# Double batches of leftover matmuls, and a beginning with whole loads on one queue

## The chip, the cores and the metric

The kernel runs on one core of a Trainium2 chip. The metric is device time in microseconds (us) of one execution; six executions of the kernel before took 2045.05 to 2046.72 us, with a median of 2046.22. The core has five engines with a queue each that run side by side: PE (TensorE, matmuls and weight loads), DVE (VectorE), ACT (ScalarE), POOL (GpSimd) and SP (SyncE, which here only issues DMAs; ACT issues some too).

## The reference

The input x has 4096 rows, 32 fields and 16 numbers per field. Two layers follow each other. Each forms all products of two fields, mixes them with a weight matrix, adds a bias, and normalizes each output channel over rows and numbers:

```python
def _cin_layer(out, x, W, b, gamma, beta):
    r, _, e = x.shape
    h = jnp.einsum('rne,rfe->rnfe', out, x).reshape(r, -1, e)
    h = jnp.einsum('rce,oc->roe', h, W) + b[None, :, None]
    return _batchnorm(h, gamma, beta)
h1 = _cin_layer(x, x, W1, b1, g1, beta1)
out, direct1 = (h1[:, :64], h1[:, 64:])
direct2 = _cin_layer(out, x, W2, b2, g2, beta2)
agg = jnp.concatenate([direct1, direct2], axis=1)
return agg.sum(axis=-1)
```

W1 is 128 x 1024 (32 x 32 field pairs), W2 is 128 x 2048. The mean and the variance of layer one are needed before layer two can multiply, so the two layers are two stages of the kernel.

## The kernel before

The change lies in stage one alone, which is layer one; it fills the first 490 of the 2043 us. The 65,536 columns (rows times numbers) are cut into 128 tiles of 512 columns; `t` counts them, and `s = t % GROUP` is the place in a group of eight.

Because both operands of a pair are x, the pairs (i, j) and (j, i) share one product, and their weights are added once at the start: `w1_sb = w1_sb + w1m_sb` on POOL (L312), in pieces of one, one, two and two of six chunks. A tile needs four products of 128 partitions by 512 columns (the main part, `z`, chunks m = 0 to 3) and 16 products of fields that lie 16 apart (the leftovers). The leftovers fill only 32 partitions for a tile, so those of four tiles are packed into one 128-partition array: one load `r` per group holds the leftovers of all eight tiles of the group (32 partitions hold two tiles, and the weight chunks 4 and 5 have zeros for the other one), and DVE multiplies it once to `zr` (L373, `leftovers`).

For each tile the work goes like this:
- SP issues the loads of `a` and `b` (512 KB each, L294 in `load_main`), one tile ahead in the text; four buffers of each mean that the loads of tile t wait until DVE has used tile t - 4. The first tile's loads are in halves. The weights `w1` and `w1m` are loaded on ACT's queue (L308, L309).
- DVE multiplies `z = a * b` (L387 `multiply_main`; the first two tiles by chunks, L396 `multiply_chunk`). There are four buffers of `z`.
- PE runs four matmuls on `z` with `w1_sb` into one PSUM bank (L428), 128 rows and 128 columns of weights each.
- At tiles with s = 0 and s = 4 PE first runs `add_leftovers` (L380): four matmuls of 32 rows each, in four different row groups, one for each of the next four tiles. They start the accumulation in these four banks. The first two tiles are the exception: they get theirs at the end (`begun`).
- `finish(t - 1)`, in the text right behind tile t's matmuls, evicts the bank of the tile before: ACT writes `e` with the bias (L352), DVE takes its statistics (L115), ACT writes the half that layer two needs (`kept`, L355, stored to DRAM by a DMA on ACT's queue) and the half that is only summed (`ed`, L358); every second tile DVE sums `ed` (L364 `sum_direct`).

PSUM has eight banks. Stage one takes six for the tiles (`psum`, bufs=6); the other two (`factors`) hold the warm-up and are used in stage two. Buffers of one: `r` and `zr`. Buffers of two: `e` and `ed`.

The order on each engine's queue is drawn up by the framework from the dependences and from the order in which the text emits the instructions: of those that it reckons ready, the one emitted first goes first. So a product can stand ahead of statistics that are emitted earlier but ready later (in the trace the product of tile 40 stands ahead of the statistics of tile 36). Where the text has `issue_after(x)`, the instruction comes behind x on its engine. Once drawn up, each queue runs strictly in order.

Some work for stage two is mixed in by tile number: the weights of layer two (load at t = 6, combined by DVE at t = 20), differences of fields (`EARLY`: loads at 14 + 24g, negated and summed on ACT and DVE behind it, stored at 37 + 24g), and the first loads of stage two (t = 75, 83, 91, 99, 107, 115).

The last four tiles (`ENDING`) are done by halves of the output channels, the half that layer two needs first, so that its statistics can be finished (L505 to L519 on DVE and ACT), while PE does the other half (L461). `add_leftovers_halves` adds their leftovers from the group's `zr` with chunk 5. A small matmul `keep_ps` spreads the scale and shift over partitions (its operand is `blocks`, L519), and stage two begins (L698).

Before all this PE runs `BEGIN` = 3 matmuls on ones (L239), whose result nobody reads, while the first loads are on their way.

## Time and profile before

| what | value |
|---|---|
| median of six executions | 2046.22 us |
| the profiled execution | 2045.05 us |
| its span, first to last instruction | 2043.3 us |
| mean granted clock of PE | 0.998 of full |
| PE busy | 2027.5 us |
| DVE busy | 1959.0 us |
| POOL busy, nearly all in stage two | 1486.4 us |
| first matmul on a tile | 8.22 us |
| end of main matmuls of tile 123 | 474.1 us |
| begin of stage two on PE | 490.48 us |

The page lists the busy time of each engine, then the chain that ended last: from the last instruction back to what released it, again and again, so that the shares show which engine set the end. Below it stand groups of instructions by line with their count, busy time, mean ns of one, and how long the engine was idle before them and who ended that. PE is the matmuls, PEld the weight loads that run beside them. In the records, a matmul of f32 shows as two, because it goes over the array in two passes, and the name `w_sb` stands for `w1_sb` in stage one. "xN" is a count of records. A DMA's time to landing includes its wait in the queue.

### The profile page before, as it was taken

The page shows a single profiled execution, that of the slowest core. Times are in us where ns is not written, and L with a number is a line of the kernel's source. Part 1 is how long each engine was busy: PE and PEld are TensorE (multiplying, and loading weights), DVE is VectorE, ACT ScalarE, POOL GpSimd, SP SyncE. Part 2 cuts the span into 40 slices and gives each one's busy share as a digit, 9 for nine tenths or more (in the row PEclk, how much of TensorE's full clock was granted, in tenths as well). Part 3 has the DMA queues.
Part 4 walks back from the last instruction along what each step waited for, and adds up shares of the span by engine and source line. Part 5 has one row for each costly group of instructions (what it writes and reads, how often), then busy time and mean ns, then how long its engine had stood idle before and what let it go on. Part 6 is the DMA issues. An engine that isn't in the chain of part 4 may idle for free.

```text
span 2043.3 us, 24467 instructions
## 1 busy us (share of the span) xinstructions
PE 2027.5 (99%) x8500; PEld 885.3 (43%) x8500; DVE 1959.0 (96%) x1521; ACT 1186.1 (58%) x1914; POOL 1486.4 (73%) x525
## 2 busy tenths in 40 slices
PE   9999999999999999999999999999999999999997
PEld 3444444443344444444444444444444444444443
DVE  8998987998999999999999999999999999999997
ACT  4555554554566666655665656556656565566564
POOL 0000000002999999999999999999999999999996
PEclk9999999999999999999999999999999999999999
DMA  9999999996777777777776777777767777777661
GB/s 391 379 346 371 348 359 355 358 390 188 176 176 181 174 175 180 190 174 188 174 177 166 174 173 178 175 183 177 176 167 174 173 173 183 181 177 175 169 162 42
DMA packets 112380, 440.70 MB, mean 216 GB/s; under 512 B 13056, under 2 KB 13056, under 8 KB 103808
## 3 DMA queue, kind: packets, MB, share of 16 engines
q1 hardware_dynamic: 105840, 418.43, 73.6%
q10 hardware_dynamic: 6416, 20.72, 2.7%
q8 instruction: 66, 1.08, 0.2%
q14 instruction: 58, 0.48, 0.1%
HBM read 417.07 MB, written 22.02 MB: 215 GB/s over the span
## 4 chain that ended last, share of the span: by engine, by line
PE 98%; DVE 1%; issue 0%; POOL 0%; DMA 0%; ACT 0%; DVEq 0%; ACTq 0%; POOLq 0%
PE x L698 74%; PE ps L428 21%; PE ps L380 2%; PE ps L461 1%; DMA w1m_sb<-in_w1m 0%; POOL t L714 0%; DVE zz L667 0%; DVE d L934 0%; ACT u L659 0%; DVE both L662 0%; POOL t L703 0%; ACT both L659 0%; DVE d L833 0%; DVE t L662 0%; POOL w_sb L312 0%
## 5 line engine op out<-in xcount | busy, mean ns | idle before, releaser
L714 POOL TENSOR_TENSOR t<-zz,t 128x2048 f32<-128x2048 f32 (+1 forms) x260 | 1163.0, 4474 | 20.6 <-DVE t L662 0.9
L698 PE MATMUL x<-t,s_sb 128*64 128x512 f32 x2040 | 958.3, 592 | 0.4 <-POOL t L714 0.4
L698 PE MATMUL x<-zz,s_sb 128*64 128x512 f32 x2048 | 934.8, 592 | 0.0
L698 PE MATMUL x<-zz,w_sb 128*64 128x512 f32 x2056 | 760.2, 592 | 0.0
L703 POOL TENSOR_TENSOR t<-zz 128x512 f32<-128x512 f32 x255 | 327.1, 1283 | 516.8 <-DVE zz L667 516.3
L667 DVE TENSOR_TENSOR zz<-f,bx 128x2048 f32<-128x2048 f32 x255 | 582.3, 2283 | 19.7 <-ACT f L659 19.7
L659 ACT ACTIVATE f<-a,keep 128x512 f32<-128x512 f32 x512 | 398.2, 778 | 342.6 <-DVE zz L667 294.7
L667 DVE TENSOR_TENSOR zz<-f,b 128x2048 f32<-128x2048 f32 x255 | 582.3, 2284 | 0.1
L698 PEld LDWEIGHTS x<-t,s_sb 128*64 128x64 f32 x2040 | 279.2, 137 | 486.2 <-issue 457.6
L698 PE MATMUL x<-t,w_sb 128*64 128x512 f32 x1020 | 479.3, 592 | 0.0
L428 PE MATMUL ps<-z,w_sb 128*128 128x512 f32 x992 | 434.7, 596 | 1.3 <-POOL w_sb L312 1.2
L698 PEld LDWEIGHTS x<-zz,s_sb 128*64 128x64 f32 x2048 | 279.5, 137 | 247.8 <-issue 240.3
L387 DVE TENSOR_TENSOR z<-a,b 128x2048 f32<-128x2048 f32 (+1 forms) x127 | 288.2, 2270 | 43.0 <-PE ps L428 20.6
L428 PEld LDWEIGHTS ps<-z,w_sb 128*128 128x128 f32 x992 | 185.7, 190 | 248.9 <-issue 228.6
L698 PEld LDWEIGHTS x<-zz,w_sb 128*64 128x64 f32 x2056 | 238.9, 137 | 121.4 <-issue 119.4
L659 ACT ACTIVATE b<-zz 128x512 f32<-128x512 f32 x255 | 152.5, 598 | 187.1 <-DVE zz L667 187.0
L352 ACT ACTIVATE e<-ps,bn_sb 128x512 f32<-128x512 f32 x124 | 85.2, 687 | 214.7 <-PE ps L428 167.5
L662 DVE TENSOR_TENSOR t<-zz,b 128x512 f32<-128x512 f32 x255 | 173.3, 680 | 0.4
L698 PEld LDWEIGHTS x<-t,w_sb 128*64 128x64 f32 x1020 | 139.6, 137 | 0.0
L596 ACT ACTIVATE unread<-e,center 128x512 bf16<-128x512 f32 x122 | 86.3, 707 | 0.0
L358 ACT ACTIVATE ed<-ps,bn_sb 64x512 f32<-64x512 f32 x124 | 84.8, 684 | 2.3
L115 DVE BATCH_NORM_STATS2 stats<-e 128x6 f32<-128x512 f32 x124 | 84.9, 686 | 0.0
(103 smaller groups left out, 867.5 us busy)
## 6 DMA issues: line engine op xcount, KB each, us to landing
a<-h SPq DMA_DIRECT2D x256, 512.0 KB, 4.6
b<-in_xb SPq DMA_DIRECT2D x64, 1024.0 KB, 9.4
a<-in_xa SPq DMA_DIRECT2D x127, 512.0 KB, 7.2
b<-in_xb SPq DMA_DIRECT2D x127, 512.0 KB, 8.2
bx<-in_xb SPq DMA_DIRECT2D x64, 512.0 KB, 9.3
bx<-x SPq DMA_DIRECT2D x64, 512.0 KB, 10.9
h<-kept ACTq DMA_DIRECT2D x64, 256.0 KB, 5.7
r<-in_xr SPq DMA_DIRECT2D x16, 512.0 KB, 8.9
```

The source lines that it names most:

```text
L115: nc.vector.bn_stats(self.stats[:, self.at, :], h)
L352: nc.scalar.activation(e, ps, AF.Identity, bias=b1)
L358: done = nc.scalar.activation(ed[to, :], ps[KEEP:, :], AF.Identity, bias=b1[KEEP:])
L387: return nc.vector.tensor_tensor(z[:, k], a.rearrange("p (a t) -> p a t", a=2)[:, k].unsqueeze(2).to_broadcast([P, n, 2, T]), b.rearrange( ...
L428: nc.tensor.matmul(pss[t], w1_sb[:, m, :], z[:, m // 2, m % 2, :], start=t < FIRST and m == 0, stop=t >= FIRST and m == 3,)
L596: return nc.scalar.activation(unread, e[:, s], AF.Square, bias=center[:, s], accum_out=squares[:, s, c : c + 1])
L659: return queue("act", lambda: nc.scalar.activation(to, source, AF.Identity, **scale_bias))
L662: return dve(lambda: nc.vector.tensor_tensor(to, x, y, ALU.add))
L667: dve(lambda: nc.vector.tensor_tensor(z, a, b.rearrange("p (k q) t -> p k q t", k=2), ALU.mult))
L698: queue("pe", lambda: nc.tensor.matmul(self.of[x], w, b, start=start, stop=stop))
L703: queue("pool", lambda: nc.gpsimd.tensor_tensor(t2[:, 0], z[:, 1, 0], z[:, 0, 0], ALU.add))
L714: queue("pool", lambda: nc.gpsimd.tensor_tensor(t14[:, k, q], z[:, 2 + k.start : 2 + k.stop, q], twice[:, k, q], ALU.subtract))
```

## The change

The leftovers of tiles 8g - 4 to 8g - 1 and of tiles 8g to 8g + 3 are now added in one go, at tile 8g: eight matmuls behind each other. The first four end the accumulation of tiles that have had their main matmuls (`ends_with_leftovers`), the second four start that of tiles that are to come. The packing of `xr` on the host is moved by four tiles to fit, with a 17th group for the last four tiles; their leftovers are multiplied in the ending, and use chunk 4. As tiles now stay open longer, they use all eight banks (`bank`: six of `psum`, and the two of `factors` for the tiles with t % 8 = 6 and 7), and they are evicted four tiles later: `finish(t - 4)` in place of `finish(t - 1)`, with two at tiles 120 and 121 and `finish(t - 2)` at 122 and 123. The load of the next `r` moves from s = 4 to s = 1 (and to t = 3 for the second one).

At the beginning, the first tile's loads are whole like all others. The weights of both orders of a pair come in one array, `w1_both` (four main chunks, 512 KB) and `left_both` (two chunks of leftovers, 256 KB), loaded on SP's queue: a and b of tile 0, main weights, a and b of tile 1, weights of leftovers, then `r`. DVE adds chunk 0 behind its first product; POOL adds chunk 1, then 2 and 3, then the leftovers'. There are four warm-up matmuls in place of three.

```diff
--- before.py
+++ after.py
@@ -60,7 +61,7 @@
 LAST = 4
 STAGES = (3, 0, 1, 2)
 DIFF = 16
-BEGIN = 3
+BEGIN = 4
 
 FIRST = 2
 
@@ -282,34 +283,17 @@
         def load_main(t):
             a = lpool.tile([P, 2 * T], FP, tag="a", name="a")
             b = lpool.tile([P, 2 * T], FP, tag="b", name="b")
-
-            def load(to, part, n):
-                at = part * T
-                if to is a:
-                    at += xa.offset + t * FIELDS * 2 * T
-                    source = bass.AP(xa.tensor, at, [[2 * T, FIELDS], [0, 4], [1, n * T]])
-                else:
-                    at += xb.offset + (t * WRAP + 2) * T
-                    source = bass.AP(xb.tensor, at, [[T, FIELDS], [4 * T, 4], [1, n * T]])
-                return nc.sync.dma_start(to[:, part * T : (part + n) * T], source)
-
-            if t == 0:
-
-                parts = ((a, 0, 1), (b, 0, 1), (b, 1, 1), (a, 1, 1))
-            else:
-                parts = ((a, 0, 2), (b, 0, 2))
-            for part in parts:
-                last = load(*part)
-            loads.append(last)
+            nc.sync.dma_start(
+                a, bass.AP(xa.tensor, xa.offset + t * FIELDS * 2 * T, [[2 * T, FIELDS], [0, 4], [1, 2 * T]])
+            )
+            at_b = bass.AP(xb.tensor, xb.offset + (t * WRAP + 2) * T, [[T, FIELDS], [4 * T, 4], [1, 2 * T]])
+            loads.append(nc.sync.dma_start(b, at_b))
             return a, b
 
         w1_sb = wpool.tile([P, 6, P], FP, tag="w1", name="w1_sb")
-        w1m_sb = zpool.tile([P, 6, P], FP, tag="z", name="w1m_sb")
-        nc.scalar.dma_start(w1_sb, w1)
-        nc.scalar.dma_start(w1m_sb, w1m)
-
-        for k in (slice(0, 1), slice(1, 2), slice(2, 4), slice(4, 6)):
-            nc.gpsimd.tensor_tensor(w1_sb[:, k], w1_sb[:, k], w1m_sb[:, k], ALU.add)
+
+        w1_both = zpool.tile([P, 2, 4, P], FP, tag="z", name="w1_both")
+        left_both = zpool.tile([P, 2, 2, P], FP, tag="z", name="left_both")
         bn_sb = load_bn()
         w2_sb = const.tile([P, 16, P], FP, tag="w2", name="w2_sb")
         s_sb = const.tile([P, 4, 4, 2, KEEP], FP, tag="s", name="s_sb")
@@ -368,18 +352,28 @@
                 ALU.add,
             )
 
+        def multiply_leftovers(zr, r):
+            return nc.vector.tensor_tensor(zr, r[:, :T], r[:, T:], ALU.mult)
+
         def leftovers(r):
             zr = rpool.tile([P, T], FP, tag="zr", name="zr")
-            nc.vector.tensor_tensor(zr, r[:, :T], r[:, T:], ALU.mult)
+            multiply_leftovers(zr, r)
             return zr
 
-        def add_leftovers(t, zr, begun=0):
+        def bank(t):
+            pool, tag = (psum, "ps") if t % GROUP < 6 else (factors, "f")
+            return pool.tile([P, T], FP, tag=tag, name="ps")
+
+        def ends_with_leftovers(t):
+            return t % GROUP >= 4 or t < FIRST
+
+        def add_leftovers(t, zr):
 
             for k in range(4):
                 rows = slice(32 * k, 32 * (k + 1))
-                nc.tensor.matmul(
-                    pss[t + k], w1_sb[rows, 4 + t % GROUP // 4, :], zr[rows, :], start=k >= begun, stop=k < begun
-                )
+                last = ends_with_leftovers(t + k)
+                w = w1_sb[rows, 4 + (t + 4) % GROUP // 4, :]
+                nc.tensor.matmul(pss[t + k], w, zr[rows, :], start=not last, stop=last)
 
         def multiply_main(z, a, b, k):
 
@@ -396,11 +390,19 @@
             return nc.vector.tensor_tensor(z[:, k, j], a[:, to[0]], b[:, to[1]], ALU.mult)
 
         ending = NT - ENDING
-        main = [load_main(t) for t in range(FIRST)]
+
+        main = [load_main(0)]
+        nc.sync.dma_start(w1_both, w1)
+        main += [load_main(t) for t in range(1, FIRST)]
+        nc.sync.dma_start(left_both, w1_left)
+        for k in (slice(1, 2), slice(2, 4)):
+            nc.gpsimd.tensor_tensor(w1_sb[:, k], w1_both[:, 0, k], w1_both[:, 1, k], ALU.add)
+        nc.gpsimd.tensor_tensor(w1_sb[:, 4:], left_both[:, 0], left_both[:, 1], ALU.add)
         r = load_rem(0)
         for t in range(NT - ENDING):
             s = t % GROUP
-            if s == 4 and t + 4 < NT:
+            if s == 1 and t > 1 or t == 3:
+
                 r = load_rem(t // GROUP + 1)
             if FIRST <= t + 1 < NT:
                 main.append(load_main(t + 1))
@@ -411,6 +413,9 @@
                 for k in range(2):
                     for j in range(2):
                         product = multiply_chunk(z, *main[0], k, j)
+                        if t == k == j == 0:
+                            with tc.issue_after(product.ins):
+                                nc.vector.tensor_tensor(w1_sb[:, 0], w1_both[:, 0, 0], w1_both[:, 1, 0], ALU.add)
             else:
 
                 for k in (slice(0, 1), slice(1, 2)) if t == FIRST else (slice(0, 2),):
@@ -421,27 +426,34 @@
                     zr = leftovers(r)
             if s % 4 == 0:
                 for k in range(4):
-                    pss[t + k] = psum.tile([P, T], FP, tag="ps", name="ps")
-            if s % 4 == 0 and t > 0:
+                    pss[t + k] = bank(t + k)
+            if s == 0 and t > 0:
+                add_leftovers(t - 4, zr)
                 add_leftovers(t, zr)
             for m in range(4):
                 nc.tensor.matmul(
                     pss[t],
                     w1_sb[:, m, :],
                     z[:, m // 2, m % 2, :],
-                    start=t < FIRST and m == 0,
-                    stop=t >= FIRST and m == 3,
+                    start=ends_with_leftovers(t) and m == 0,
+                    stop=not ends_with_leftovers(t) and m == 3,
                 )
             if t == FIRST - 1:
-                add_leftovers(0, zr, FIRST)
-            if t > 0 and t < ending - 1:
-                evicted = finish(t - 1)
+                add_leftovers(0, zr)
+
+            if t >= ending - 2:
+                evicted = finish(t - 2)
+            elif t >= ending - 4:
+                for done in range(2 * t - ending, 2 * t - ending + 2):
+                    evicted = finish(done)
+            elif t >= 4:
+                evicted = finish(t - 4)
             if t == 20:
                 combine_weights()
                 b1_swapped = const.tile([P, 1], FP, tag="b1s", name="b1_swapped")
                 for x, y in ((low, high), (high, low)):
                     nc.scalar.activation(b1_swapped[x], b1[y], AF.Identity)
-            if t == 0:
+            if t < 4:
                 continue
             with tc.issue_after(loads[-1].ins), tc.issue_after(product.ins), tc.issue_after(evicted.ins):
                 if t == 12:
@@ -477,7 +489,7 @@
             for k in range(ENDING):
                 rows = slice(32 * k, 32 * (k + 1))
                 to = banks[k][half_of[(k + direct) % 2]]
-                matmul(to, w1_sb[rows, 5, half_of[direct]], zr[rows, :], k not in begun, k in begun)
+                matmul(to, w1_sb[rows, 4, half_of[direct]], zr[rows, :], k not in begun, k in begun)
 
         zs = []
         for k in range(ENDING):
@@ -485,6 +497,9 @@
                 main.append(load_main(ending + k + 1))
             zs.append(zpool.tile([P, 2, 2, T], FP, tag="z", name="z"))
             queue("dve", lambda: multiply_main(zs[k], *main.pop(0), slice(0, 2)))
+            if k == 0:
+                zr = rpool.tile([P, T], FP, tag="zr", name="zr")
+                queue("dve", lambda: multiply_leftovers(zr, r))
 
         with tc.issue_after(lasts["dve"].ins):
             for t in (ending - 2, ending - 1):
@@ -965,8 +980,10 @@
     n = np.arange(FIELDS)
     xa = np.stack([xt, xt[:, (n + 2) % FIELDS]], axis=2)
     xb = xt[:, np.arange(WRAP) % FIELDS]
-    xr = np.stack([xt[:, :16], xt[:, 16:]], axis=2).reshape(NT // GROUP, GROUP // 4, 4, 16, 2, T)
-    xr = xr.transpose(0, 2, 1, 3, 4, 5).reshape(NT // GROUP, P, 2, T)
+
+    xr = np.stack([xt[:, :16], xt[:, 16:]], axis=2)
+    xr = np.concatenate([xr[:4], xr, xr[-4:]]).reshape(NT // GROUP + 1, GROUP // 4, 4, 16, 2, T)
+    xr = xr.transpose(0, 2, 1, 3, 4, 5).reshape(NT // GROUP + 1, P, 2, T)
 
```

## The prediction

> **What bounds the kernel now.** I read the page first, for the engine that carries the span.
>
> ```profile
> span 2043.3 us, 24467 instructions
> PE 2027.5 (99%) x8500; PEld 885.3 (43%) x8500; DVE 1959.0 (96%) x1521; ACT 1186.1 (58%) x1914; POOL 1486.4 (73%) x525
> PE 98%; DVE 1%; issue 0%; POOL 0%; DMA 0%; ACT 0%; DVEq 0%; ACTq 0%; POOLq 0%
> ```
>
> PE is busy 99% and the chain that ended last is 98% PE. So a gain has to be PE time, and a loss has to be a hole in PE. Next I read the chain in order of time over the first 60 us, where all changed lines lie (the same pattern runs to 474 us).
>
> ```profile
> 1.29 5.25 DMA w1m_sb<-in_w1m
> ...
> 8.22 1.10 PE ps L428 x2
> 9.39 1.10 PE ps L428 x2
> 10.53 5.39 PE ps L428 x12
> 15.91 1.07 PE ps L380 x8
> 16.98 7.06 PE ps L428 x16
> ...
> 25.12 13.93 PE ps L428 x32
> 39.05 1.07 PE ps L380 x8
> 40.12 13.93 PE ps L428 x32
> ```
>
> Each f32 matmul gives two records, its two passes. From 10.53 us on PE has no hole: 32 records of main matmuls, then 8 of leftovers, again and again, 15.00 us per four tiles. The main records start 0.429 us apart (median of 924). 32 x 0.429 = 13.73, so a batch of leftovers costs 15.00 - 13.73 = 1.27 us. Its four matmuls sit in four row groups and run side by side, which is two passes, 0.86 us; the other 0.41 us is the price of going from full rows to 32-row groups and back. Then the weight loads of one batch:
>
> ```profile
> 38.98 0.31 PEld L380 LDWEIGHTS ps<-zr,w_sb 32*128 32x128 f32 x8 [0.76 <-issue]
> ```
>
> All eight loads, those of the second pass too, are over 0.31 us after the first started, while the first pass still runs in the same row groups. Last, DVE, which feeds PE (groups of lines by shape, 60 to 474 us; its waits to 520 us; the timelines at 355 us).
>
> ```profile
> L387 DVE TENSOR_TENSOR z<-a,b 128x2048 f32<-128x2048 f32 x112 | 256.2, 2288 | 41.0 <-PE ps L428 19.4 <-DMA b<-in_xb 17.6 <-PE ps L380 3.6
> L115 DVE BATCH_NORM_STATS2 stats<-e 128x6 f32<-128x512 f32 x111 | 76.2, 687 | 0.0
> L364 DVE TENSOR_REDUCE d<-ed 128x32 f32<-128x512 f32 x56 | 37.5, 669 | 0.0
> L373 DVE TENSOR_TENSOR zr<-r 128x512 f32<-128x512 f32 x14 | 9.4, 670 | 0.0
> ```
> ```profile
> 355.08 8.42 PE L428 MATMUL ps<-z,w_sb 128*128 128x512 f32 x19
> ```
> ```profile
> 355.22 2.29 DVE L387 TENSOR_TENSOR z<-a,b 128x2048 f32<-128x2048 f32 x1 [3.55 <-PE ps L380]
> ```
>
> Eight tiles cost DVE 8 x 2.288 + 8 x 0.687 + 4 x 0.669 + 0.670 = 27.2 us of PE's 30.0. Mostly DVE waits for a free z buffer and is 9 us ahead (the product of tile 40 ends at 151.09, PE starts that tile at 160.06). The thin places are the start (tile 8: 38.36 against 40.05) and tile 93: counted off, the product in the last row is tile 93's, it ends at 357.51, and PE starts the tile eight records after 355.08, at 358.62: 1.1 us. Around it the DMA share is 1.00 (330 to 360 us).
>
> **The change, part by part.**
>
> *Double batches.* Before there are 32 batches, each with its two switches; after, one single batch at tile 1, 15 double ones at tiles 8 to 120, and the ending's own: 15 pairs of switches fewer. A double batch is four passes and one pair of switches if its second half follows as the second pass of a batch follows the first: 4 x 0.429 + 0.41 = 2.13 us, against 2 x 1.27 = 2.54. That is 15 x 0.41 = **-6.1 us**. The least gain, if the joint of the halves costs a half switch (0.2 us), is 15 x 0.2 = 3.1 us.
>
> The Trainium skill, "TensorE: Matmul & The Clock Gate", Part 3, speaks against the joint: a weight load overlaps running matmuls only where its row group differs, and the second half's loads go to the row groups in use. "TensorEngine Tiling (Array Packing)", Key Properties, has only a change of tiling mode drain the array, which speaks for it. By the first I would estimate the smaller gain. The row above shows loads into groups in use, so I take the larger.
>
> *Evictions four tiles late.* Tiles whose number modulo 8 is 4 to 7 are complete only at the next double batch. Then ACT has four of them at once: 4 x 2.04 us (0.687 + 0.670 + 0.684) = 8.2 us, and DVE gets 4 x 0.687 + 2 x 0.669 = 4.1 us of their statistics and sums, ahead of the next product in its queue if they stand in the order of emission. From the batch to the end of the fourth tile behind it PE takes about 15 us; in that time DVE has four products (9.2), eight statistics and four sums (8.2), some 17 us. So in this half DVE falls back from 9 us of lead to, worked out with ACT's pace, about 3.5 us, and in the other half, which has almost only products (four in 14 us), it comes back. In the steady state this is hidden by the lead. Where the lead is gone already it is not: from tile 80 to 93 PE now saves 3 x 1.27 - 2.13 = 1.7 us against a lead of 1.1, a hole of 0.6. At the start tile 4 comes 1.27 us earlier for want of its batch, against leads of 1.7 to 2.5 up to tile 11; no hole by these numbers. For the burst of statistics meeting a late load I add 0.9. **+1.5 us**; least 0 (a product is never needed late), most 6.5, which is all of the gain: then DVE and DMA, not PE, set the pace.
>
> *Loads of leftovers moved* from the 4th to the 1st tile of a group, one earlier still at tile 3. On SP's queue the load stands ahead of the next tile's loads and waits until DVE has multiplied the old leftovers (one buffer). That product now is just behind the load's place, before it was four tiles back, so the loads of a and b queued behind it can be held up to 5 us. They have about 11 us from buffer free to product and take 7 to 8 us to land, so the product is 1 to 2 us late: covered by the lead, nothing by itself, and part of the 6.5 above. There is one load and one product (0.68) more, in the ending.
>
> *The beginning.* Before, the first two tiles' 32 records would take 13.73 / 2 = 6.87 us and end at 15.91: an effective start of 9.04, because PE waited for POOL's sums at 8.22, 9.39 and 10.53. After, the queue of SP carries a, b (512 KB each) and all weights of the first four chunks (512 KB) first: 1.5 MB; before, 1.5 MB had landed by 7.27, and from then on, in packets of 4 KB, the queue moved 1 MB per 2.5 us. I put the weights at 6.4 to 7.4. DVE adds chunk 0 (a 128x64 add took 0.22; about 0.3), so it is ready by 6.7 to 7.7; POOL's 0.46 and 1.2 us for the other chunks run beside PE's 0.86 per chunk; DVE's products take 0.69 alone and 1.2 beside POOL. The fourth warm-up matmul moves PE's free time from 6.84 by 2 x 0.853 to 8.55, unless the clock rises in it. So PE starts at about 8.6 without the later waits, **-0.4 us**; ends: -1.0 (clock up early) and +1.0 (weights at 8.5 or a late product). The skill's "Trainium Kernel Development and Optimization", Key Constraints, holds that several issuing queues only save issue time; by that one queue costs nothing but SP's 0.54 to 0.74 us per load. No row here has the two orders side by side.
>
> *The ending.* ACT has eight evictions (16.3 us) between the last double batch and the end of tile 123, 15 us; PE's next banks need tiles 116, 117, 120, 121, done by 12.4. DVE's own order is full to the end, but it sat idle 0.88 and 2.04 us before the last statistics. The final link is tight: blocks (L519) end at 486.28, PE reads them at 486.51. **0**, at most +2.
>
> The rest (1.5 ms of stage two) is untouched and moves as a whole. Sum: -6.1 + 1.5 - 0.4 + 0 = **-5.0 us**. The profiled execution took 2045.05 us (span 2043.3 and 1.75 around it), so 2040.05; it was the fastest of six, 1.17 below the median, so **2041.2** at the median.
>
> **Rivals.**
> 1. *The joint costs a half switch.* For it: no row shows two batches behind each other; against it: the row of eight loads. 2046.2 - 3.1 - 0.4 + 1.0 = 2043.7.
> 2. *The lead is eaten:* the holes take all of the gain. For it: DMA share 1.03 from 16 to 99 us, the 1.1 us at tile 93; against it: 93 waits, 174 us in all, of SP's loads for a free buffer, so the DMA has spare time. 2046.2 - 0.4 = 2045.8.
> 3. *Slower: PE waits behind every double batch* for a product that stands behind the burst of statistics on DVE. It decides from 0.43 us per batch on; at 1 us it is 15 - 6.5 = +8.5: 2054.7. For it: 17 us of DVE work in 15; against it: four z buffers and the idle half that follows.
> 4. *The beginning alone is worse,* by the 1.0 above: 2042.6, still a gain.
>
> **How the numbers follow.** Forecast 52%; rival 1 10%; rival 2 16%; rival 3 20%; rival 4 2%. A measurement here can tell about 0.2%, 4.1 us: faster is below 2042.1, slower above 2050.3. The forecast and its neighbours give faster 0.52, the rivals 1, 2 and 4 same 0.28, rival 3 slower 0.20. The forecast's own range is 2038.8 (6.1 + 1.0 with no hole) to 2043.5; to leave out no more than 2 in 10 I go to 2048.0, into the mild end of rival 3.
>
> **What the profile will show.** Right: chain pieces of L428 in 64 records and leftovers in 16 records of about 1.95 us (one switch lies in the pieces beside them), 29.6 us per eight tiles, PE without holes from about 8.6 us, stage two starting some 5 us before 490.48. Wrong in the joint: 16 records taking 2.1 us and more. Wrong in the cover: idle time of PE at L428 released by DVE z, some tiles behind a batch or near tile 93. The prediction fails if those holes repeat in every group or if the ending's link comes late.

## The result, and the profile after

The changed kernel took 2050.51 us (median of 21 executions, 2043.16 to 2055.41), against 2046.07 us for the kernel before (42 executions, 2044.82 to 2047.98). The ratio is 1.0023 with a 95% interval of 1.0017 to 1.0029: slower by 0.23%. Forecast were 2041.2 us, 2048.0 at most, and a gain. The profiled execution took 2050.69 us, near the median.

The page of the changed kernel, same three lines as before:

```profile
span 2048.9 us, 24489 instructions
PE 2027.3 (99%) x8502; PEld 892.3 (44%) x8502; DVE 1960.1 (96%) x1523; ACT 1185.8 (58%) x1914; POOL 1486.6 (73%) x524
PE 89%; DMA 5%; DVE 3%; issue 1%; ACT 1%; POOL 0%; SPq 0%; DVEq 0%; ACTq 0%; POOLq 0%
```

PE's busy time looks unchanged (2027.3 against 2027.5), although 6.15 us of it were removed: time at half clock counts as busy too (1.7 and 1.6 us of it below), the fourth warm-up matmul adds 1.1 (the warm-up ends at 8.15 us and not at 7.04), the ending 0.95, and short gaps between matmuls count in part. What tells is the chain: PE fell from 98% to 89% of it, and DMA and DVE came in. Stage two starts on PE at 496.31 us (before 490.48), 5.8 us late, and from there the two kernels are equal. So the whole loss is in stage one.

The chain in order of time over the first 80 us (start, duration, what):

```profile
2.17 7.67 DMA w_both<-in_w
...
9.86 0.30 DVE w_sb L418
...
10.20 8.83 PE ps L434 x16
...
41.77 1.93 PE ps L376 x16
43.70 27.66 PE ps L434 x64
71.36 1.93 PE ps L376 x16
```

From the third line of main matmuls on, this is what was forecast: leftovers in 16 records of 1.93 us, main matmuls in 64, eight tiles in 29.59 us and not 30.00. The joint of the two halves costs nothing. PE's weight loads at that double batch (start, duration, then what):

```profile
41.70 0.31 PEld L376 LDWEIGHTS ps<-zr,w_sb 32*128 32x128 f32 x8 [0.76 <-issue]
42.24 0.20 PEld L376 LDWEIGHTS ps<-zr,w_sb 32*128 32x128 f32 x4 [0.23 <-issue]
42.67 0.20 PEld L376 LDWEIGHTS ps<-zr,w_sb 32*128 32x128 f32 x4 [0.22 <-issue]
```

The loads of the second half come at 42.24 and 42.67, 0.43 us apart, one pass each, beside the running matmuls. The rule weighed in the prediction (the Trainium skill, "TensorE: Matmul & The Clock Gate", Part 3: only loads into other row groups overlap) would have cost here; the measurement decides against it for this pattern.

The start is worse in this execution. The main weights, third in SP's queue, land at 9.84 us, so the first tile matmul comes at 10.20 (before 8.22). And the first passes run at half clock. Windows of the changed kernel (after the busy times of the five engines stand PE's granted clock, the DMA share and GB/s):

```profile
10.00:12.00 2.00, 1.80 (x3) 0.92 (x4) 2.00 (x3) 0.00 (x0) 1.59 (x2) 0.71 1.05 416
12.00:14.00 2.00, 2.00 (x3) 0.67 (x2) 2.00 (x4) 0.00 (x0) 0.90 (x1) 0.50 1.02 416
14.00:16.00 2.00, 2.00 (x6) 0.99 (x5) 2.00 (x4) 0.00 (x0) 0.00 (x0) 0.94 1.04 424
```

The clock column loses 2 x (0.29 + 0.50 + 0.06) = 1.7 us. The first batch of leftovers comes at 19.04 us, 3.1 us later than before (15.91); two small holes before tiles 3 and 4 add 0.66. Other executions start otherwise, with the old beginning too; see "What the beginning costs".

The largest loss is around tiles 90 to 92. PE's timeline there (a hole before tile 90, one before tile 92), the chain up to the product of tile 91 (350.08), and DVE's timeline from there to the product of tile 92:

```profile
344.82 1.88 PE L434 MATMUL ps<-z,w_sb 128*128 128x512 f32 x4
349.05 8.66 PE L434 MATMUL ps<-z,w_sb 128*128 128x512 f32 x16 [2.35 <-DVE z L381]
360.36 2.81 PE L434 MATMUL ps<-z,w_sb 128*128 128x512 f32 x6 [2.65 <-DVE z L381]
```
```profile
314.52 13.18 DMA a<-in_xa
...
327.76 11.13 DMA a<-in_xa
...
338.91 10.98 DMA b<-in_xb
...
350.08 2.30 DVE z L381
```
```profile
350.08 2.29 DVE L381 TENSOR_TENSOR z<-a,b 128x2048 f32<-128x2048 f32 x1 [1.09 <-DMA b<-in_xb]
352.29 1.28 DVE L116 BATCH_NORM_STATS2 stats<-e 128x6 f32<-128x512 f32 x2
...
354.69 0.67 DVE L356 TENSOR_TENSOR zr<-r 128x512 f32<-128x512 f32 x1
356.06 0.69 DVE L116 BATCH_NORM_STATS2 stats<-e 128x6 f32<-128x512 f32 x1 [0.69 <-ACT e L336]
357.33 0.69 DVE L348 TENSOR_REDUCE d<-ed 128x32 f32<-128x512 f32 x1 [0.58 <-ACT ed L342]
357.94 2.28 DVE L381 TENSOR_TENSOR z<-a,b 128x2048 f32<-128x2048 f32 x1
```

PE waits twice for DVE's product, for two reasons. The products of tiles 90 and 91 wait for their loads, which land at 346.2 and 349.9 us; the loads in the chain take 11 to 13 us from issue to landing (the medians from 60 to 474 us are 6.9 for `a` and 7.8 for `b`). The product of tile 92 (357.94) does not wait for its loads: SP issued them at 340.43 and 342.84, and they had landed by 353.3. It stands in DVE's queue behind the burst of statistics and sums that the double batch sets off, with `zr` among them and two short waits for ACT's evictions. From the end of tile 91's product to the end of tile 92's this takes 7.8 us, where PE needs 3.4 for a tile. From the starts of the records around them the two holes are 2.5 and 2.8 us. The 16 records after the first hole take 8.66 us where 15 x 0.429 + 0.59 = 7.0 would do: half clock again, 1.6 us. Together 6.9 us.

Last, the ending. What PE's line for the last four tiles waited for, in the changed kernel (us, times):

```profile
  DVE z L381: 0.8, 1
  ACT ed L342: 0.8, 1
```

Each of these waits pulls apart a pair of 64-column matmuls that otherwise run side by side (one pass, 0.43 us). The 64 records of this piece take 13.44 us and not 12.49: 0.95 us. The other profiles with double batches have the same 0.95 but for two: batches_alone, where PE also waits 1.13 us for a product, takes 2.25 us more than before from the end of tile 123 to stage two, and r_at_five, with 1.45.

Sum, against the profiled execution of before: -6.15 (15 x 0.41) + 3.1 + 0.66 + 6.9 + 0.95 = +5.5 us; the spans differ by 2048.9 - 2043.3 = 5.6.

### The profile page after: what moved, and what is told of

It is laid out like the page before. It is cut to its first block, busy times and chain, and to the rows that moved or that the text cites. A ratio compares the mean times of both kernels' runs of the same rounds, so it can differ in the third digit from the quotient of the medians.

```text
span 2048.9 us, 24489 instructions
## 1 busy us (share of the span) xinstructions
PE 2027.3 (99%) x8502; PEld 892.3 (44%) x8502; DVE 1960.1 (96%) x1523; ACT 1185.8 (58%) x1914; POOL 1486.6 (73%) x524
## 3 DMA queue, kind: packets, MB, share of 16 engines
q8 instruction: 66, 1.08, 0.2%
## 4 chain that ended last, share of the span: by engine, by line
PE 89%; DMA 5%; DVE 3%; issue 1%; ACT 1%; POOL 0%; SPq 0%; DVEq 0%; ACTq 0%; POOLq 0%
PE x L713 74%; PE ps L434 13%; DMA b<-in_xb 2%; DMA a<-in_xa 2%; DVE z L381 2%; PE ps L376 1%; PE ps L473 1%; DVE stats L116 0%; DMA w_both<-in_w 0%; DMA h<-kept 0%; ACT ed L342 0%; POOL t L729 0%; ACT e L336 0%; ACT kept L339 0%; DVE d L348 0%
```

## The experiments

Each kernel was timed beside the kernel before (2045.99 to 2046.40 us in the several series; the ratio is to that of its own series). "The hole" is the one at tiles 90 to 92. A useful measure is the lead: from the end of DVE's product of a tile to PE's first matmul on it. Near zero means that PE waits. Leads come from one profiled execution of each kernel; that of r_later was its fastest. The times are medians, the ratios and their intervals follow the means, and the two differ where executions spread.

| kernel | median us | ratio, 95% interval | lead at tiles 84, 88, 90, 91, 92 (us) |
|---|---|---|---|
| before | 2046.07 | | 8.97, 6.95, 3.46, 3.57, 4.02 |
| changed | 2050.51 | 1.0017 to 1.0029 | 3.49, 0.34, 0.05, 1.74, 0.15 |
| begin_alone | 2046.30 | 0.9993 to 1.0011 | 8.80, 8.17, 5.89, 6.53, 7.09 |
| batches_alone | 2050.14 | 1.0011 to 1.0028 | 3.08, 1.28, 0.06, 0.05, 0.15 |
| r_at_two | 2049.72 | 1.0001 to 1.0022 | 1.99, 0.06, 0.06, 0.06, 0.15 |
| r_later | 2042.12 | 0.9979 to 0.9996 | 3.54, 5.32, 3.84, 4.81, 0.69 |
| r_on_act | 2047.57 | 0.9998 to 1.0016 | 3.27, 1.54, 0.06, 0.05, 0.15 |
| r_once | 2040.90 | 0.9966 to 0.9986 | 3.54, 6.30, 5.31, 6.29, 2.17 |

In the profiles of all thirteen kernels with double batches and `r` not at s = 5, the product of tile 92 ends 7.6 to 7.8 us behind that of tile 91 (kernel before: 4.2). PE needs 3.4 us for a tile, so this step takes 4.1 to 4.4 us off the lead, whatever happened before; a lead under that at tile 91 becomes a hole at tile 92.

### Each half of the change alone

**begin_alone**: the kernel before with the new beginning only. All else is as before, single batches included.

```diff
-BEGIN = 3
+BEGIN = 4
-        main = [load_main(t) for t in range(FIRST)]
+        main = [load_main(0)]
+        nc.sync.dma_start(w1_both, w1)
+        main += [load_main(t) for t in range(1, FIRST)]
+        nc.sync.dma_start(left_both, w1_left)
...
+                            with tc.issue_after(product.ins):
+                                nc.vector.tensor_tensor(w1_sb[:, 0], w1_both[:, 0, 0], w1_both[:, 1, 0], ALU.add)
```

> The kernel before with the new beginning alone (whole first loads, weights on SP's queue behind them, chunk 0 added on DVE, four warm-up matmuls), batches and evictions as before. Theory: the beginning itself costs about 3.9 us: the first matmul on a tile at about 10.2 us in place of 8.2, its first 3.4 us at half clock (about 1.9 us), small holes at tiles 3 and 4 less than that because tile 4 still has its batch in front. So about 2049.5 us, stage two's first matmul at about 494, and no hole of PE near tile 90, where the lead comes back to 9 us before. Rival: the beginning is cheap (+1 at most, 2047) and what was lost in the changed kernel's first 30 us comes from the batches.

Measured: 2046.30 us, ratio 1.0002 (0.9993 to 1.0011). The chain of the profiled execution (2047.03 us):

```profile
2.16 7.42 DMA w_both<-in_w
...
9.95 2.05 PE ps L420 x4
```

The first tile matmul is as late as in the changed kernel (9.95 us), but without half clock, and stage two starts 1.8 us late. In the median nothing shows: the rival held for the time.

**batches_alone**: the changed kernel with the old beginning (the reverse of the diff above).

> The changed kernel with the old beginning: double batches, late evictions and the moved load of leftovers alone. Theory: -6.1 for the batches, +0.95 for the ending, and the hole near tiles 90 to 92 stays (some 5 to 7 us with its stretch at half clock), since it comes from a lead of 3 to 4 us in place of 9 meeting a stretch that the DMA limits: 2046 to 2048 us. Rival: the hole comes from the beginning (other DMA semaphores, shifted loads): then no hole, 2041 us, as forecast.

Measured: 2050.14 us, ratio 1.0019 (1.0011 to 1.0028): the whole loss, and 2 us more than my theory allowed. The profile has the double batches at 1.93 us as forecast, and the hole: PE idle until 356.85 us for tile 92, half clock after it. (This execution also has half clock at the start, with the old beginning, and the wait in the ending named above.) So the double batches do what was forecast and something that came with them takes more than they give.

### Is it the start?

**weights_on_act** puts both loads of weights on ACT's queue, **warm_longer** has seven warm-up matmuls.

```diff
-        nc.sync.dma_start(w1_both, w1)
+        nc.scalar.dma_start(w1_both, w1)
...
-        nc.sync.dma_start(left_both, w1_left)
+        nc.scalar.dma_start(left_both, w1_left)
```
```diff
-BEGIN = 4
+BEGIN = 7
```

> The changed kernel with the two loads of weights on ACT's queue, all else as changed. Theory: the single queue is what makes the weights late (landed at 9.85 us in the changed kernel, 6.5 before); on a second queue they land by 7 us, PE starts when the first product is there, about 9.4, and its idle time is short enough that the clock stays: 2 to 3 us off the changed kernel, about 2048. Rival: bytes, not queues, set the landing: a and b then land later by as much as the weights land earlier, PE starts at about 10 us as before, no change (2050.5).

> The changed kernel with seven warm-up matmuls in place of four, so that PE is busy until about 10.6 us. Theory: the half clock from 10.9 to 14.3 us is the answer to PE's idle 2 us before 10.2; without the idle time it does not come, the first two tiles take 6.9 us in place of 8.8, and PE starts 0.4 us later: 1.5 us off the changed kernel, about 2049. Rival: the clock falls at a fixed time whatever PE does: no gain, or 0.4 us lost.

Measured: 2051.39 us (ratio 1.0021, 1.0003 to 1.0040) and 2052.39 us (1.0026, 1.0017 to 1.0034). The seven executions of weights_on_act spread from 2041.04 to 2057.95. Both profiles have a good start: no half clock, and the first batch of leftovers at 16.01 and 16.25 us, where the changed kernel has 19.04. In the medians nothing is gained. The chains of weights_on_act and of warm_longer up to tile 92 (each one's last line):

```profile
357.22 0.14 issue
357.35 12.66 PE ps L434 x25
```
```profile
359.81 0.14 issue
359.94 10.40 PE ps L434 x20
```

357.35 and 359.94, against 360.36 in the changed kernel and 356.85 in batches_alone. The start does not order these times: warm_longer wins 2.8 us there and keeps 0.4 of them at tile 92, weights_on_act keeps 3.0, and batches_alone, whose first batch came at 17.97, has tile 92 first of all. PE reaches tile 92 and waits in each of them; what sets the time is when the product of tile 91 ends, plus the burst.

### Is it stage two's first loads?

Six loads for stage two are mixed into stage one from tile 75 on. Around them the transfers slow down: in the changed kernel 399 GB/s from 300 to 310 us, then 269, 383 and 310, at a DMA share of 1.02 to 1.03. **spread** moves them apart, with double batches and the old beginning; **spread_before** does the same to the kernel before.

```diff
-    EARLY += [(75, lambda: early.append(load_b(0))), (83, lambda: early.append(load_bx(0)))]
-    EARLY += [(91 + 8 * k, lambda i=i: early.append(load_a(0, i))) for k, i in enumerate(STAGES)]
+    EARLY += [(47, lambda: early.append(load_b(0))), (55, lambda: early.append(load_bx(0)))]
+    EARLY += [(at, lambda i=i: early.append(load_a(0, i))) for at, i in zip((70, 78, 102, 110), STAGES)]
```

> The changed kernel with the old beginning, and stage two's first loads moved away from tiles 75 to 91: b at 47, bx at 55, the four a at 70, 78, 102 and 110, in place of 75, 83, 91, 99, 107, 115. Theory: the hole of PE at tiles 88 to 92 comes from slow transfers (b, bx and the differences' loads move 200 to 300 GB/s where the tiles' own move 420) packed into sixteen tiles, which take more than the lead of 3 to 4 us; spread out, the hole goes, with it its 3.4 us of half clock: about 6 us off the 2050.1 of the kernel without it, 2042 to 2044, and PE without a hole from 60 to 470 us. Rival: the hole is the double batches' own (burst of statistics on DVE); it stays, or moves to other tiles, and the time stays at 2049 to 2051.

> The kernel before with the same loads of stage two moved as in the run called spread. Theory: PE has no hole there to begin with (lead of 1.1 us left at tile 93), so the time is the same, 2046.4, and the lead at tile 93 comes out at 5 us or more. Rival: stage two's loads cost PE time in the kernel before as well: 1 us or more off.

Measured: 2047.86 us (ratio 1.0007, 0.9999 to 1.0016) and 2045.13 us (0.9998, 0.9989 to 1.0007). For spread this lies between theory and rival; it may help a little (its interval overlaps that of batches_alone), and the hole goes where the loads went. PE's timeline of spread:

```profile
204.29 15.67 PE L442 MATMUL ps<-z,w_sb 128*128 128x512 f32 x32 [1.90 <-DVE z L398]
...
266.71 1.53 PE L442 MATMUL ps<-z,w_sb 128*128 128x512 f32 x3 [1.30 <-DVE z L398]
```

These are tiles 52 and 68, fifth in their groups like tile 92: four tiles behind a double batch, where the lead is lowest. In spread_before the lead is 8 to 9 us from tile 36 to 108 (9.07 at tile 93, where the kernel before has 1.11), so it is these loads that make tile 93 thin before the change; the time stays the same, since a lead that is never used up costs nothing.

Whether a short lead alone opens a hole, without double batches, stays untested: a kernel before with three `z` buffers (before_z3) deadlocks and has no time; its ending holds four products at once.

### The place of the loads of leftovers

The change also moves the load of `r`. A load emitted at the turn s of the group stands in SP's queue ahead of the loads of tile s + 1. **r_later** takes batches_alone and moves it by two tiles.

```diff
-            if s == 1 and t > 1 or t == 3:
+            if s == 3:
```

> The changed kernel with the old beginning, and the load of the next leftovers issued at the 4th tile of a group in place of the 2nd, so that SP never waits for the product of the leftovers just before it. Theory: this wait is not what makes the hole (at 360 us the queue is full, the DMA is the limit): 2049 to 2051, hole near tile 90 within 1.5 us of before. Rival: SP's queue stands behind this load for some 5 us in each group, the loads of a and b come late and eat the lead: without it 2043 to 2046 and the hole gone or under 2 us.

My theory fell here and the rival held: 2042.12 us, ratio 0.9988 (0.9979 to 0.9996), 8.0 us faster than batches_alone and faster than the kernel before. The chain around tile 92 has no DMA in it:

```profile
334.17 1.93 PE ps L393 x16
336.10 27.66 PE ps L442 x64
363.77 1.93 PE ps L393 x16
```

SP's timeline in the changed kernel and in r_later:

```profile
330.35 0.59 SPq L191 DMA_DIRECT2D xs<-in_xb  x1
332.24 0.33 SPq L280 DMA_DIRECT2D r<-in_xr  x1
332.67 0.54 SPq L286 DMA_DIRECT2D a<-in_xa  x1
336.83 0.54 SPq L290 DMA_DIRECT2D b<-in_xb  x1
```
```profile
322.87 0.59 SPq L191 DMA_DIRECT2D xs<-in_xb  x1
324.81 0.54 SPq L295 DMA_DIRECT2D a<-in_xa  x1
325.39 0.60 SPq L295 DMA_DIRECT2D b<-in_xb  x1
328.30 0.53 SPq L295 DMA_DIRECT2D a<-in_xa  x1
328.87 0.62 SPq L295 DMA_DIRECT2D b<-in_xb  x1
330.04 0.33 SPq L280 DMA_DIRECT2D r<-in_xr  x1
```

In the changed kernel `r` (512 KB) follows `xs` (512 KB) directly, and both stand ahead of the loads of tile 90. Behind them SP issues nothing for 4 us, 3.6 of them a wait for the landing of a `b`; pauses as long stand in r_later too (344.45 to 349.21 us). In r_later two tiles' loads go in between, and the loads of tile 91 have landed at 339.2 us, where batches_alone has them at 346.7.

**after_r_later**: the same edit in the changed kernel itself, with its new beginning.

> The changed kernel with one thing undone: the loads of leftovers stand two tiles later in SP's order (before the loads of the 4th tile of a group, not of the 2nd). Theory: their place in SP's queue makes the holes near tiles 90 to 92, and the new beginning adds only what it cost alone in the profile (+1.5 to 1.8, up to +3.9 with the half clock). So 2042.1 (the same edit with the old beginning) + 1.5 to 3.9 = 2043.6 to 2046.0, no idle time of PE over 1 us between 300 and 365 us. Rival: the late start of the new beginning eats the lead as well, the holes stay, and the time stays at 2048.5 to 2051.

Measured: 2046.97 us, ratio 1.0003 (0.9994 to 1.0012), 3.5 us faster than the changed kernel, but 1 us above the range expected; one hole of 2.2 us stays at tile 92 (353.36 us), behind a lead of 2.04 at tile 91.

**before_r_early**: the kernel before, with its loads of `r` moved to where the change has them.

```diff
-            if s == 4 and t + 4 < NT:
+            if (s == 1 and t > 1 or t == 3) and t + 7 < NT:
```

> The kernel before with one thing changed: the loads of leftovers three tiles earlier in SP's order (the place of the changed kernel), single batches as they were. Theory (the place alone costs, where the lead is thin): the 1.1 us of lead at tile 93 are gone, a hole of 1 to 3 us with its half clock, 2047.0 to 2050. Rival: the place costs only together with the bursts behind double batches, which take the lead down to 3 us in every group; here the lead is 9 us, so 2046.1 within 0.5, no hole.

The rival held: 2046.46 us, ratio 1.0002 (0.9993 to 1.0010), no hole, a lead of 8.97 us at tile 84 and 3.42 at 92. The early place costs only together with the double batches, whose burst takes the lead at the fifth tile of a group from 9 us to between 2.9 and 3.8, and to 1.1 to 2.2 at tiles 20, 44 and 68 (changed kernel). These three, like tile 92, come four to six tiles behind loads of `xs`.

**r_at_two** and **r_at_five**: other places, double batches and old beginning. In r_at_five the last of the loads falls away, since the loop ends before its turn, and the last four tiles take the leftovers of the group before.

```diff
-            if s == 1 and t > 1 or t == 3:
+            if s == 2 and t > 2 or t == 3:
```
```diff
-            if s == 1 and t > 1 or t == 3:
+            if s == 5:
```

> Double batches with the old beginning, the loads of leftovers before the loads of the 3rd tile of a group: between the place of the change (2050.1) and the place two tiles later (2042.1). Theory (the load collides in the queue with stage two's first loads, and each tile of distance gives its loads 1.2 to 2 us): between the two, 2043.5 to 2048.5. Rival (a step: only the wait for DVE's product of the old leftovers costs, and it is over by the 3rd tile): 2041 to 2043.

> Double batches with the old beginning, the loads of leftovers before the loads of the 6th tile of a group, two tiles later again. Theory (the later in SP's queue the better, as long as the product of the leftovers is not late): 2040.5 to 2042.5. Rival (the product of leftovers now comes late on DVE, in front of the products of the last tiles of a group and of the batch): a wait ahead of some batches, 2044 to 2048.

Measured: 2049.72 us (ratio 1.0012, 1.0001 to 1.0022; executions from 2041.88 to 2052.43) and 2065.75 us (1.0101, 1.0087 to 1.0115). One tile later hardly helps the median (2049.72 lies above both ranges), two take away 8.0 us, four cost 15.6 us more than the early place, far beyond both ranges. The last has a plain cause. DVE's timeline of r_at_five:

```profile
330.09 0.69 DVE L373 TENSOR_TENSOR zr<-r 128x512 f32<-128x512 f32 x1 [6.08 <-DMA r<-in_xr]
```

In DVE's order `zr` stands ahead of the product of the fifth tile of a group, four tiles before the batch that uses it. With s = 3, `r` stands in SP's queue ahead of the loads of just that tile: the latest of the places run at which DVE need not wait (s = 4 was not run). With s = 5 it stands two tiles behind them, and DVE waits for `r`, 47.6 us in all before 13 products of leftovers.

**r_later_spread**: r_later and spread together.

> Double batches, old beginning, loads of leftovers two tiles later, and stage two's first loads spread over tiles 47 to 110: both neighbours of the collision moved apart. Theory: no hole is left in any execution, so the whole 6.1 us of the batches: 2046.1 - 6.1 + 0.5 (first tiles, ending) = 2040 to 2041.5, and the executions lie within 2 us of each other. Rival: the spread loads only move the thin place elsewhere (with the early place of the leftovers' load they gave a hole at 202 us): 2042 to 2045.

Measured: 2042.55 us, ratio 0.9986 (0.9977 to 0.9994): no different from r_later, executions from 2040.14 to 2046.44, and not within 2 us of each other. At tile 92 the lead is now 3.2 us, but at tile 68 it is 0.7: the rival held, the thin place moves.

### Bytes or place

**r_on_act** issues the early loads of `r` on ACT's queue. **r_once** loads the leftovers for the first two groups only and multiplies the second group's data again: 15 loads are left out, and DVE and PE have the same work.

```diff
-                nc.sync.dma_start(r, bass.AP(xr.tensor, xr.offset + g * P * 2 * T, [[2 * T, P], [1, 2 * T]]))
+                nc.scalar.dma_start(r, bass.AP(xr.tensor, xr.offset + g * P * 2 * T, [[2 * T, P], [1, 2 * T]]))
```
```diff
-            if s == 1 and t > 1 or t == 3:
+            if t == 3:
```

> Double batches with the old beginning, the loads of leftovers at the place of the change in the text, but issued on ACT's queue: they stand ahead of no load of a or b in SP's queue, and the same bytes move. Theory (what costs is that they stand ahead of the tiles' loads in one queue that is drained in order): 2041 to 2044, as with the place two tiles later (2042.1). Rival (what costs is the bytes in that stretch, on whatever queue, since the transfer engines are full from 270 to 355 us): 2047 to 2051.

> Double batches with the old beginning, the leftovers loaded for the first two groups only, so that 15 loads of 512 KB are left out, and the later groups multiply the second group's data again: the instructions of DVE and PE stay. Theory (the load of leftovers ahead of the tiles' loads is the difference between 2050.1 and 2042.1): no hole, 2040 to 2042, executions within 3 us. Rival (the bursts of statistics and the first loads of stage two make the holes without it): 2044 to 2048.

Measured: 2047.57 us (ratio 1.0007, 0.9998 to 1.0016) for r_on_act, in the rival's range. Off SP's queue the loads may cost less than in it (its interval and that of batches_alone overlap), but the hole stays, at 356.78 us for tile 92. The run changes the time as well as the queue: the `r` ahead of the hole goes out at 318.5 us, where batches_alone has 329.7. So it shows that leaving SP's queue is not enough, and not that the place in it is worth nothing. r_once: 2040.90 us (0.9976, 0.9966 to 0.9986; executions within 2.3 us), 9.2 us faster than batches_alone. That is what double batches and the ending give by themselves (2046.18 - 6.15 + 0.95 = 2040.98), so the loads of leftovers are the whole difference. The end of stage one in r_once's chain:

```profile
364.80 1.93 PE ps L393 x16
366.73 27.66 PE ps L442 x64
...
469.44 13.43 PE ps L481 x64
```

No hole there, and the ending's 0.95 us is in it as well. Windows of the changed kernel and of r_later (columns as above):

```profile
300.00:345.00 45.00, 45.00 (x128) 19.32 (x127) 35.22 (x31) 19.40 (x30) 0.00 (x0) 1.00 1.03 346
345.00:362.00 17.00, 12.00 (x24) 4.86 (x24) 12.93 (x12) 8.46 (x14) 0.00 (x0) 0.90 0.92 309
```
```profile
300.00:345.00 45.00, 45.00 (x128) 19.33 (x127) 38.74 (x35) 22.04 (x35) 0.00 (x0) 1.00 1.03 359
345.00:362.00 17.00, 17.00 (x41) 7.52 (x40) 16.39 (x14) 9.00 (x14) 0.00 (x0) 1.00 1.02 417
```

Up to 345 us the DMA engines are full in both and move nearly as much. Then r_later goes on at 417 GB/s, while the changed kernel falls to 309 with a DMA share of 0.92. A hole feeds itself: a late product frees its buffers late, so the next loads start late too. In the changed kernel SP issues no load between 353.26 and 360.25 us, when the product of tile 92 has just ended (360.22).

### What the beginning costs

**later_on_act**: the changed kernel with `r` at s = 3 and the weights on ACT's queue. **after_r_once**: the changed kernel, new beginning and all, with the leftovers loaded as in r_once. Both edits are shown above.

> The changed kernel with two edits: loads of leftovers two tiles later, and both loads of weights on ACT's queue; the first tile's loads stay whole, the adds stay chunk by chunk. Theory (of the beginning, the single queue is what costs, since it brings the first tile's data 1 to 2 us late and the lead never gets that back before tile 92): 2041 to 2043.5, as with the whole old beginning (2042.1). Rival (the whole loads of the first tile, or the adds by chunk, cost as well): 2045 to 2047.5, as with the whole new beginning (2047.0).

> The changed kernel, new beginning and all, with the leftovers loaded for the first two groups only (15 loads of 512 KB left out, the second group's data multiplied again): no early load of leftovers is left, so what the beginning costs by itself must show against 2040.9 of the same with the old beginning. Theory (its late start, 1.5 to 3.9 us in the profiles, is paid in full once no hole hides it): 2042.4 to 2044.8. Rival (it costs only through the lead at tile 92, which here is not used up): 2040.5 to 2041.5.

Measured: 2045.16 us (ratio 0.9991, 0.9982 to 1.0000) and 2043.03 us (0.9986, 0.9977 to 0.9995). By after_r_once against r_once (2043.03 - 2040.90) the new beginning costs about 2.1 us with double batches when no load of leftovers is in the way (1.8 by the means; the two intervals overlap). With `r` at s = 3 it costs 4.9 (2046.97 against 2042.12; 3.0 by the means, and these intervals overlap at their ends), part of it through the lead: in the profiles it leaves 2.30 us at tile 88 and 0.15 at tile 92, where the old one leaves 5.32 and 0.69. With the early `r`, where the hole eats whatever the start wins, 0.4; with single batches (begin_alone) nothing. Of the 4.9 the single queue seems to be 1.8 (2046.97 - 2045.16), but these two intervals overlap as well; how the rest divides between the whole loads and the adds by chunk stays open.

The half clock at the start belongs to neither beginning. With the new one on SP's queue the first batch of leftovers comes at 19.04 us in the changed kernel, at 17.42 in begin_alone, 16.49 in after_r_later and 16.23 in after_r_once, the last three without half clock. The old one has 15.91 in the kernel before and 17.97 in batches_alone, with a granted clock of 0.50 from 10 to 12 us.

## Why the prediction was wrong, step by step

- **Double batches, -6.1: right.** 29.59 us per eight tiles, 15 times 0.41. Rival 1 (the joint) is out: 1.93 us for 16 records, second-half loads beside running matmuls. That r_once takes 2040.9, where the forecast had 2041.2, is in part luck: its other terms are +0.95 for the ending and nothing for a hole or a beginning, where the forecast had +1.5 and -0.4.
- **Evictions four tiles late: the mechanism right.** "DVE falls back from 9 us of lead to about 3.5": measured 2.88, 3.78, 3.12, 3.78, 3.13 and 3.49 us at tiles 28, 36, 52, 60, 76 and 84 of the changed kernel, but 1.08, 2.03 and 2.17 at tiles 20, 44 and 68, which the forecast did not set apart. "No hole by these numbers" at the start was off by the 0.66 at tiles 3 and 4.
- **Loads of leftovers moved, "covered by the lead, nothing by itself": this is the step that failed.** The early place costs 8.0 us with the old beginning (2050.14 against 2042.12; 6.7 by the means) and 3.5 with the new (2050.51 against 2046.97; 4.2 by the means), both against s = 3; the old place s = 4 was not run with double batches. I had priced the right instruction on the right queue, but let the lead cover its delay of "1 to 2 us", in the paragraph after the one in which that lead shrinks to 3.5; and I left it out of the sum at the one place where I had found a lead of 1.1. The profiles have a lead of 4.81 us at tile 91 with the late place and of 0.05 with the early one. Nor was it the wait that I had named (for DVE's product of the old leftovers): in the changed kernel that wait shows for two loads only, 8.1 us in all and both long before the hole, and in batches_alone for none. What costs is 512 KB ahead of the tiles' loads of a group that has `xs` and stage two's first loads in it as well.
- **Holes, "+1.5, most 6.5": too small.** The 0.9 in it "for the burst of statistics meeting a late load" named what happens at tile 92 and missed its size: the two holes are 5.3 us and draw 1.6 of half clock. "Most 6.5, which is all of the gain" was no bound: nothing in the sum stops a hole at the size of the gain, since late products make late loads. With `r` at s = 3 the hole of 0.6 that I had worked out for tile 93 is a lead of 0.69 at tile 92 in the fastest execution, so that term was about right without the moved load.
- **The beginning, -0.4: not what came.** I put the weights at 6.4 to 7.4 us by the rate of "1 MB per 2.5 us"; they landed at 9.84. From 4 to 6 and from 6 to 8 us the changed kernel moved 229 and 307 GB/s, the kernel before 296 and 379, and that rate would be some 420. The bound "+1.0 (weights at 8.5)" was too near. In the profile it is +3.1, of which 1.7 are half clock; by the runs 2.1 us with double batches, and nothing with single ones. Half clock after the idle time behind the warm-up was no term of mine at all.
- **The ending, 0 (at most +2): +0.95**, within its bounds, in the changed kernel and most others; batches_alone, with 2.25, was outside them.
- **Rivals.** Rivals 2 and 3 both had a part. Rival 2 (the lead is eaten, transfers set the pace) is what happened up to tile 91, but its price, the gain and no more, was too low. Rival 3 (PE waits for a product that stands behind the burst of statistics) is the hole at tile 92, but in one group and not in all fifteen, since elsewhere the lead outlasts the burst. Against rival 2 I had counted SP's 174 us of waits for a free buffer as spare time of the DMA. Its share shows little: 0.93 to 1.03 in all windows of the kernel before from 16 to 459 us, and 1.03 from 300 to 345 us after the change. A slip without weight: the forecast's own lower end, 2038.8, is 2039.1 by its terms (2046.2 - 7.1).

What stays open is why one tile's shift of `r` (r_at_two) does almost nothing for the median and two do all. Its executions, 2041.88 to 2052.43, suggest that a run either falls into the hole or misses it. The 4.1 to 4.4 us that the burst takes would make such a step, but no run here shows what decides on which side of it an execution falls.

r_later and r_later_spread beat both kernels: against the before of their series by 0.12% and 0.14% in the mean (2.5 and 3.0 us), and by 4.0 and 3.4 us in the median.

## What to carry to other kernels

When a change spends a lead (here 9 us down to 3.5, for bursts on DVE), price every transfer that it moves against the lead that is left at the thinnest place, not against the lead of before. Here the early load alone cost nothing (before_r_early) and the double batches alone gained 4.0 us (r_later); together they lost 3.7. Where the profile names a DMA as the releaser of a late product, look up that tile's own loads: at tile 92 they had landed 4.7 us earlier, and the product stood in its queue behind other work. A load that is moved earlier in an in-order queue is not free because it is off the critical path; of the places run here the best was just ahead of the loads that its first reader runs next to, which the readers' own order gives. And a wide spread of executions went here with a used-up lead at tile 92 (12 us in the changed kernel; 3 in the one before, and 2.3 in r_once, which keep 4.02 and 2.17 there).

## What the runs showed of the hardware

- A hole of PE may or may not bring half clock. Idle times of 2.35 us before 349.05 us did (1.6 us more), of 2.65 us before 360.36 us did not, in the same execution. At the start, 2.05 us of idle were followed by half clock, and the longer idle time in begin_alone (first matmul at 9.95 us, 2.74 us idle) was not. A hole of 1.90 us had it too (spread, tile 52: granted clock 0.67 from 204 to 208 us), and so had the five at tile 92 of 3.5 us and more. The Trainium skill, "TensorE: Matmul & The Clock Gate", Part 1, has a free-running window of about 3.4 us, which fits that the outcome depends on more than the length; its "≥1 idle window" would not lead one to expect it at 2.35 us.
- The same instructions start at different times: with the new beginning on SP's queue and four warm-up matmuls the first tile matmul came at 10.20, 9.95, 9.02 and 8.76 us in four profiled kernels, with the old one at 8.11 to 8.94 in eleven.
- Busy transfer engines tell little of what they move: at shares of 1.02 to 1.03 the changed kernel moved from 269 to 417 GB/s in windows of 10 us.
